# Branch hints, two final splits in other buffers, and all outputs from SyncE: an edge-convolution GNN on one core

## The chip, the cores and the metric

The kernel runs on one core of a Trainium2 chip. The metric is the device time of one execution in microseconds (us). The execution that was profiled is one of the runs; its span, from the first to the last instruction of the core, is a little shorter than its device time.

## The reference

A graph network with pre-normalisation over N = 2500 nodes with D = 256 features and E = 80,000 edges sorted by target node. There are three layers, then one product of all four feature sets with `Wf`, and the input is added at the end.

```python
def edge_conv(x, src, dst, W, b):
    m = concat([x[dst], x[src] - x[dst]]) @ W + b
    return segment_sum(m, dst) / maximum(segment_count(dst), 1)

h = maximum(layernorm(x), 0); xs = [h]
for W, b in ((W0, b0), (W1, b1), (W2, b2)):
    h = relu(edge_conv(h, src, dst, W, b)); xs.append(h)
out = x + concat(xs) @ Wf + bf          # Wf is 1024 x 256
```

## The kernel before

The program has two parts. `by_windows` does the whole computation under the assumption that the edges of a window of nodes fit into a fixed number of slots; it also writes a flag, `missing`, that says whether an edge was left out. Afterwards `gnn_kernel` loads the flag on every engine (`nc.values_load`, line 1425) and a branch on it (`tc.If`, line 1426) leads into `general`, a slower way of computing everything, or past it. With these inputs the flag is zero, so every engine jumps over the instructions of `general`, waits until what it issued is done, and meets the others at the barrier that ends the program (line 1450).

In `by_windows` the nodes are 20 tiles of 128. Edge counts are made as a dense matrix in five column groups, and a layer is a product of that matrix with the features. Most engine calls go through the helper `InOrder`, which keeps each engine's instructions in the order of the source; that is why nearly all of them carry line 282. A float32 operand that needs full precision is held as three reduced-precision parts (`high`, `low`, `across`). `Split` makes these parts for the two node tiles 2q and 2q+1 of `hT`: ScalarE (ACT) writes `high`, VectorE (DVE) makes `low` with a subtraction and `across` with a scalar_tensor_tensor. `Forms` does the like for a weight; `times` multiplies a split with the forms, 6 matmuls for a node tile. The parts lie in a pool `stage` with four buffers (tiles named "staged"), or, for the first layer, in the pool `ready` with seven buffers of half that size, from which `block()` also hands out the blocks of the count matrix that the layers multiply with (tiles named "block").

The part around the change is the end of the last layer and the final product:

- Each layer after the first runs a stream of 70 steps; after step n the function `tick(n)` slips other work in. In the last layer it makes four splits (steps 49, 56, 63 and 65) and the forms of the last part of `Wf` (64 to 67).
- The final loop runs over `order = [8, 9, 0, 1, 2, 3, 7, 6, 5, 4]`, whose entries q are pairs of node tiles; `i` counts them. For each pair TensorE (PE) writes both tiles' products into PSUM: 12 matmuls from a split, or 8 plain float32 matmuls for q = 2 and 7 (`PLAIN`). DVE then adds each tile to `acc` (`add_to_acc`), and SyncE (SP) issues the transfer of the tile to the output in HBM. In the last two pairs (`i >= Q - 2`) ACT issues the second tile's.
- At the end of round i the loop makes the splits of the next three entries that are not there yet. In effect the split of q = 3 comes after round 2, of 6 after round 4, of 5 after round 5 and of 4 after round 6. Each takes a `stage` buffer, which an earlier split must have freed.

The transfers go through eight semaphores in turn (100, 102, 103, 104, 106, 107, 109, 110). After the branch SP waits for each of these, then for a list of other semaphores, then goes to the barrier. DVE, PE and ACT wait after the branch for their own last instruction only. The barrier is led by GpSimd (POOL).

Of the kernel before, what the change touches and what calls it, by code (L numbers as in the profile page):

```python
# [8 lines left out]
F32 = mybir.dt.float32  # L9
I32 = mybir.dt.int32  # L10
AF = mybir.ActivationFunctionType
# [260 lines left out]
class InOrder:  # L272


    def __init__(self, tc, engine):
        self.tc, self.engine = tc, engine
# [37 lines left out]
def by_windows(ctx: ExitStack, tc: tile.TileContext, x, src, dst, Ws, bs, Wf, bf, out, missing):  # L314
    nc = tc.nc
    PE, DVE, ACT, POOL, SP = nc.tensor, nc.vector, nc.scalar, nc.gpsimd, nc.sync
    PEo, DVEo, POOLo, ACTo, SPo = (InOrder(tc, e) for e in (PE, DVE, POOL, ACT, SP))
    P = 128
    N, D = x.shape
# [4 lines left out]
    L = len(Ws)  # L324
    DC = D // P
# [22 lines left out]
    Q = NT // 2  # L348
# [23 lines left out]
    def bank():  # L372
        return ps[-1].tile([P, 512], F32, name="bank")


    acc = const.tile([P, NT, D], F32, name="acc")
    hT = const.tile([P, DC, NP], F32, name="hT")
# [66 lines left out]
    def load_wb(l, queue=SP):  # L444
        new_raw(l)
        ws[l] = (wts[l] if l == 1 else wpool.tile([P, DC, D], F32, name="wt")), raws[l][:, :, 0, :]
        queue.dma_start(ws[l][1], Ws[l][D:2 * D, :].rearrange("(c p) d -> p c d", p=P))
# [3 lines left out]
    def load_wt(l, queue=SP):  # L451
        queue.dma_start(wts[l] if l == 1 else ws[l][0], Ws[l][0:D, :].rearrange("(c p) d -> p c d", p=P))

    def load_wf(l, queue=SP):
        if l == L:
            new_raw(l)
        wfs[l] = raws[l][:, :, 1, :]
        queue.dma_start(wfs[l], Wf[l * D:(l + 1) * D, :].rearrange("(c p) d -> p c d", p=P))
# [22 lines left out]
    def load_b(l, queue=SP):  # L481
        queue.dma_start(brow[PAD:PAD + 1, l % 2, :], bs[l].rearrange("(o d) -> o d", o=1))
# [110 lines left out]
    parts = {}  # L593
# [320 lines left out]
    order = """  # L914
# [39 lines left out]
    DOWN = 1.0 - 0.5 / E12  # L954

    splits, coming = {}, []

    def block():
        return ready.tile([P, 2, 512], F32R, name="block")

    def flat(l):
        return raws[l].rearrange("p c t d -> p c (t d)") if l < L else wfs[l]

    class Split:

        def __init__(self, q, parts):
            h = hT[:, :, 2 * q * P:(2 * q + 2) * P]
            high, low, across = self.parts = [p.rearrange("p (c n) -> p c n", c=DC) for p in parts]
            ACTo.activation(high, h, AF.Copy, scale=DOWN)
            DVEo.tensor_sub(low, h, high.bitcast(F32))  # L970
            DVEo.scalar_tensor_tensor(across, low.bitcast(F32), -E12, high.bitcast(F32), op0=OP.mult, op1=OP.add)
            splits[q] = self

    class Forms:

# [35 lines left out]
    def split_own(g, c):  # L1011
# [4 lines left out]
        DVEo.tensor_sub(low, h, high.bitcast(F32))  # L1016
        DVEo.scalar_tensor_tensor(across, low.bitcast(F32), -E12, high.bitcast(F32), op0=OP.mult, op1=OP.add)

    def first_forms():
        DVEo.tensor_sub(ws[1][0], ws[1][0], ws[1][1])  # L1020
        yield
        coming.append(Forms(flat(1), [flat(1)[:, c, :] for c in range(DC)]))
        coming[0].high()
        coming[0].low()
        yield
        coming[0].across()
        coming[0].last()
        yield
        for q in range(2):
            two = [block().rearrange("p c n -> p (c n)") for _ in range(2)]  # L1030
            Split(q, [two[0][:, :2 * D], two[0][:, 2 * D:], two[1][:, :2 * D]])
            yield
        for t in range(0, NT, 5):
            DVEo.tensor_add(acc[:, t:t + 5, :], acc[:, t:t + 5, :], bf_sb.unsqueeze(1).to_broadcast([P, 5, D]))
            yield
# [68 lines left out]
    def combine(to, x):  # L1104
        DVEo.tensor_sub(to[:, M3:S5 + 1, :], x[:, 1::2, :], x[:, 0:2, :])
        DVEo.tensor_sub(to[:, S2, :], to[:, M3, :], x[:, 3, :])
        DVEo.tensor_add(to[:, M4, :], to[:, S2, :], x[:, 2, :])
# [10 lines left out]
    def add_to_acc(t, po):  # L1118
        DVEo.scalar_tensor_tensor(acc[:, t, :], po, share[:, t:t + 1], acc[:, t, :], op0=OP.mult, op1=OP.add)
# [161 lines left out]
    def load_alone(k, order):  # L1281
        c = order[2 * k] // 2
        st = stage.tile([P, 8 * GS], BF16, name="staged").rearrange("p (t n) -> p t n", n=GS)[:, :4, :]
        SPo.dma_start(st, a_dram[alone][:, 4 * c:4 * c + 4, :])
        loaded[k] = st
# [42 lines left out]
    PLAIN = (2, 7)  # L1328
    LAG = 2
    orders = [None, list(range(Q)), [8, 9, 0, 1, 2, 3, 7, 6, 5, 4], [8, 9, 0, 1, 2, 3, 7, 6, 5, 4]]  # L1330
    def split(q):
        tile_ = stage.tile([P, 4 * GS], F32R, name="staged")
        Split(q, [tile_[:, k * 2 * D:(k + 1) * 2 * D] for k in range(3)])

    for l in range(1, L):
        order = orders[l]
        lone = Alone(l, order)
        if l == 1:
            load_alone(0, order)
            split(order[2])  # L1340
        pending = []
        stream = Stream(l)
        for i in range(Q + LAG):
            if 0 < i <= Q:
                lone.make(i - 1)
            if i < Q:
                q = order[i]
                n = Nodes(l, q)
                n.multiply(splits.pop(q), coming[0])
                if i + AHEAD_H < Q and i % 2 == 1:  # L1350
                    load_alone((i + 1) // 2, order)
                n.parts()
                n.combine()
                if i + AHEAD_H < Q and order[i + AHEAD_H] not in splits:
                    split(order[i + AHEAD_H])
                pending.append(n)
            if i and pending:
                pending.pop(0).sums()
            if 0 < i <= DC:
                lone.own(i - 1, 0)  # L1360
            if i >= LAG:
                lone.multiply(i - LAG)
            if i == Q - 1:
                load_alone(Q // 2 - 1, order)
                stream.load(3)
        stream.make(2)
        lone.end()
        turn_of[1] = 0
        if l + 1 < L:
            load_b(l + 1, SPo)  # L1370
            load_wb(l + 1, SPo)
            load_wt(l + 1, SPo)
        load_wf(l + 1, SPo)
        after = orders[l + 1]

        def tick(n):
            if n == 3:
                combine(wsum, ws[l][0].rearrange("p c (o n) -> p (c o) n", o=2))
            if n == 40 and l + 1 < L:
                DVEo.tensor_sub(ws[l + 1][0], ws[l + 1][0], ws[l + 1][1])  # L1380
            if n in (49, 56):
                split(after[(n - 49) // 7])
            if n == 63 and l + 1 < L:
                load_alone(0, after)
            if n in ((65,) if l + 1 < L else (63, 65)):
                split(after[2 + (65 - n) // 2])
            if n == 64:
                raw = flat(l + 1)
                coming[:] = [Forms(raw, [raw[:, c, :] if l + 1 < L else raws[L][:, c, 0, :] for c in range(DC)])]
                coming[0].high()  # L1390
                coming[0].low()
            if n == 66:
                coming[0].across()
            if n == 67:
                coming[0].last()

        stream.run(tick)

    order = orders[L]
    for i, q in enumerate(order):  # L1400
        po = bank()
        po = [po[:, :D], bank()[:, :D] if i == Q - 1 else po[:, D:]]
        for k in range(2):
            if q in PLAIN:
                for c in range(DC):
                    PEo.matmul(po[k], hT[:, c, (2 * q + k) * P:(2 * q + k + 1) * P], wfs[L][:, c, :],
                               start=(c == 0), stop=(c == DC - 1))
            else:
                times(po[k], splits[q], k, coming[0])
        for k in range(2):  # L1410
            t = 2 * q + k
            add_to_acc(t, po[k])
            n = P if t < NT - 1 else LAST
            (ACTo if i >= Q - 2 and k else SPo).dma_start(out[t * P:t * P + n, :], acc[:n, t, :])
        for k in order[i + 1:i + 4]:
            if k not in splits and k not in PLAIN:
                split(k)


def gnn_kernel(tc: tile.TileContext, x, src, dst, Ws, bs, Wf, bf, out):  # L1420
    nc = tc.nc
    with tc.tile_pool(name="flag", bufs=1) as flag:
        missing = flag.tile([1, 1], I32, name="missing")
        by_windows(tc, x, src, dst, Ws, bs, Wf, bf, out, missing)
        again = nc.values_load(missing, min_val=0, max_val=1)
        with tc.If(again > 0):
            general(tc, x, src, dst, Ws, bs, Wf, bf, out)


# [26 lines left out]
```

## Time and profile before

| what | value |
|---|---|
| median device time, 3 runs | 478.93 us (478.14 to 479.45) |
| profiled execution, device time | 478.33 us |
| its span | 476.4 us |
| mean granted TensorE clock | 0.995 |
| PE busy | 463.5 us, 97% of the span |
| DVE busy | 380.9 us, 80% |
| ACT busy | 310.8 us, 65% |
| transfers `out_dram<-acc` issued by SP, by ACT | 18, 2 |
| last DVE addition ends | 468.3 us |
| from there to the end of the span | 8.1 us |

The profile tells engine time by groups of instructions. An engine name with a q (ACTq, SPq, PEldq) is that engine's sequencer: branches, semaphore waits, register loads and the issue of transfers, which are not counted as busy. Times within the span are counted from its first instruction.

### The profile page before, as it was taken

To read this page: it belongs to the slowest core of one execution; us is meant where nothing else is said; L and a number is where in the kernel's file an instruction comes from. 1 tells how busy PE (TensorE), PEld (TensorE's weight loads), DVE (VectorE), ACT (ScalarE), POOL (GpSimd) and SP (SyncE) were. 2 spreads that over 40 slices of the span, in tenths; PEclk is the share of its full clock that TensorE was granted. 3 is DMA by queue.
4 is the path that set the end of the run, shared out by engine and by line. 5 is a ranking of instruction groups with operands and counts; after the bars stand their busy time and mean duration, and the time that the engine had idled before them with its cause. 6 is when DMAs were issued, how large, how long until landed. Compare 5 with 4: busy or idle time off the path is not lost.

```text
span 476.4 us, 7357 instructions
## 1 busy us (share of the span) xinstructions
PE 463.5 (97%) x2739; PEld 365.9 (77%) x2739; DVE 380.9 (80%) x699; ACT 310.8 (65%) x543; POOL 42.7 (9%) x66
## 2 busy tenths in 40 slices
PE   8999999999999999999999999999999999999992
PEld 4787888787877888868887867877788787687691
DVE  8988988799898872599986848876999685669883
ACT  5776687685754441577869858766877886587330
POOL 2664014300101001000000000000000000000000
PEclk9999999999999999999999999999999999999997
DMA  8310084990824608441187542011124764120032
GB/s 279 96 46 1 1 163 70 193 216 14 178 42 89 131 1 179 95 131 43 45 291 258 182 160 89 1 44 45 43 54 158 289 207 151 77 88 0 1 128 95
DMA packets 21779, 52.11 MB, mean 109 GB/s; under 512 B 1943, under 2 KB 12134, under 8 KB 21734
## 3 DMA queue, kind: packets, MB, share of 16 engines
q1 hardware_dynamic: 14662, 33.67, 21.5%
q0 software_dynamic: 5856, 16.51, 18.1%
q10 hardware_dynamic: 1216, 1.37, 0.9%
q8 instruction: 23, 0.38, 0.3%
q14 instruction: 22, 0.18, 0.1%
HBM read 36.08 MB, written 15.46 MB: 108 GB/s over the span
## 4 chain that ended last, share of the span: by engine, by line
PE 86%; DVE 7%; POOL 2%; DMA 2%; issue 1%; SPq 0%; DVEq 0%; POOLq 0%
PE bank L282 82%; PE pz L282 3%; DVE acc L282 2%; DMA acc<-in_x_dram 2%; POOL acc L282 1%; DVE staged L282 1%; DVE st L282 1%; POOL es L282 1%; DVE zl L282 0%; POOL ed L282 0%; DVE mv L282 0%; DVE tmp L282 0%; PE turned L282 0%; DVE rs L282 0%; DVE kn L282 0%
## 5 line engine op out<-in xcount | busy, mean ns | idle before, releaser
L282 ACT CAST block<-staged 128x1008 fp32r<-128x1008 bf16 x120 | 117.8, 1032 | 17.1 <-DVE staged L282 6.3
L282 PE MATMUL bank<-block,zh 128*128 128x504 f32 (+1 forms) x200 | 83.7, 419 | 0.0
L282 PE MATMUL bank<-a,zh 128*128 128x504 f32 (+1 forms) x200 | 81.7, 409 | 0.0
L282 ACT CAST a<-bank 128x480 fp32r<-128x480 f32 (+1 forms) x105 | 54.5, 561 | 39.0 <-PE bank L282 37.1
L282 PE MATMUL bank<-a,zl 128*128 128x504 f32 (+1 forms) x200 | 77.8, 389 | 0.0
L282 PE MATMUL bank<-block,zl 128*128 128x504 f32 (+1 forms) x200 | 77.3, 387 | 0.0
L282 DVE TENSOR_TENSOR one_m<-iota_m,key_m 128x2048 bf16<-128x2048 bf16 (+2 forms) x55 | 64.3, 1169 | 9.9 <-PE bank L282 9.7
L282 PE MATMUL bank<-block,sh 128*128 128x504 f32 x160 | 69.0, 431 | 0.0
L282 PE MATMUL bank<-block,staged 128*128 128x512 f32 (+1 forms) x312 | 67.2, 365 | 0.6 <-DVE staged L282 0.5
L282 PE MATMUL bank<-block,sl 128*128 128x504 f32 x160 | 62.6, 391 | 0.0
L282 PEld LDWEIGHTS bank<-block,staged 128*128 128x128 f32 x312 | 52.3, 188 | 11.9 <-DVE staged L282 2.1
L282 DVE TENSOR_TENSOR one_n<-iota_n,key_n 128x960 bf16<-128x960 bf16 (+2 forms) x110 | 51.4, 508 | 0.0
L282 DVE TENSOR_TENSOR block<-staged 128x1008 fp32r<-128x1008 bf16 x40 | 46.9, 1204 | 5.5 <-PE bank L282 4.2
L282 PEld LDWEIGHTS <-one_m 128*128 128x128 bf16 x834 | 37.4, 97 | 13.6 <-issue 7.6
L282 PEld LDWEIGHTS bank<-block,zh 128*128 128x128 f32 x200 | 37.6, 188 | 10.8 <-issue 2.5
L282 PEld LDWEIGHTS bank<-block,zl 128*128 128x128 f32 x200 | 37.6, 188 | 10.6 <-issue 3.5
L282 PE MATMUL bank<-one_n,one_m 128*128 128x120 bf16 x834 | 44.7, 204 | 0.1
L282 PEld LDWEIGHTS bank<-a,zh 128*128 128x128 f32 x200 | 37.8, 189 | 6.4 <-issue 0.2
L282 PEld LDWEIGHTS bank<-a,zl 128*128 128x128 f32 x200 | 37.8, 189 | 6.3 <-issue 0.2
L282 DVE TENSOR_TENSOR staged<-staged 128x1008 bf16<-128x1008 bf16 x40 | 27.1, 678 | 17.3 <-ACT block L282 16.9
L282 PE MATMUL pz<-wbf,hT 128*128 128x256 f32 x160 | 38.7, 387 | 0.9 <-DMA wbf<-in_L_gnn_Wf_dram 0.7
L282 PEld LDWEIGHTS bank<-block,sh 128*128 128x128 f32 x160 | 30.1, 188 | 10.4 <-issue 3.5
(163 smaller groups left out, 611.8 us busy)
## 6 DMA issues: line engine op xcount, KB each, us to landing
staged<-a_dram SPq DMA_DIRECT2D x52, 504.0 KB, 4.2
a_dram<-a POOLq DMA_DIRECT2D x20, 630.0 KB, 10.8
out_dram<-acc SPq DMA_DIRECT2D x17, 128.0 KB, 1.7
acc<-in_x_dram POOLq DMA_DIRECT2D x3, 640.0 KB
wbf<-in_L_gnn_Wf_dram SPq DMA_DIRECT2D x4, 256.0 KB
acc<-in_x_dram SPq DMA_DIRECT2D x1, 896.0 KB
acc<-in_x_dram ACTq DMA_DIRECT2D x1, 768.0 KB
wbf<-in_L_gnn_W_dram SPq DMA_DIRECT2D x3, 256.0 KB, 6.6
```

The source lines that it names most:

```text
L282: return self.tc.keep_in_program_order(call(*args, **kwargs))
```

## The change

Three things change, and nothing in what is computed.

1. At the head of the program a branch hint for the branch on `missing` is put on PE, DVE and ACT. It is one instruction on each, ahead of all their other work, and says that the jump past `general` is likely. SP and POOL get none.
2. The final splits come sooner. The one for q = 6 is begun in step 68 of the last layer's stream (only ACT's `high`); its DVE part follows after round 0. The split of 3 is made after round 1, of 5 after round 2 and of 4 after round 3. Those of 6 and 3 no longer lie in `stage` but take two `ready` blocks each, as the first layer's two splits do.
3. SP issues all 20 output transfers; ACT issues none.

```diff
-        def __init__(self, q, parts):
-            h = hT[:, :, 2 * q * P:(2 * q + 2) * P]
-            high, low, across = self.parts = [p.rearrange("p (c n) -> p c n", c=DC) for p in parts]
-            ACTo.activation(high, h, AF.Copy, scale=DOWN)
-            DVEo.tensor_sub(low, h, high.bitcast(F32))
+        def __init__(self, q, parts, whole=True):
+            self.h = hT[:, :, 2 * q * P:(2 * q + 2) * P]
+            self.parts = [p.rearrange("p (c n) -> p c n", c=DC) for p in parts]
+            ACTo.activation(self.parts[0], self.h, AF.Copy, scale=DOWN)
+            if whole:
+                self.rest()
+            splits[q] = self
+
+        def rest(self):
+            high, low, across = self.parts
+            DVEo.tensor_sub(low, self.h, high.bitcast(F32))
             DVEo.scalar_tensor_tensor(across, low.bitcast(F32), -E12, high.bitcast(F32), op0=OP.mult, op1=OP.add)
-            splits[q] = self
...
+    def split_in_blocks(q, whole=True):
+        two = [block().rearrange("p c n -> p (c n)") for _ in range(2)]
+        return Split(q, [two[0][:, :2 * D], two[0][:, 2 * D:], two[1][:, :2 * D]], whole)
...
         def tick(n):
+            if n == 68 and l + 1 == L:
+                begun.append(split_in_blocks(6, False))
...
-            (ACTo if i >= Q - 2 and k else SPo).dma_start(out[t * P:t * P + n, :], acc[:n, t, :])
-        for k in order[i + 1:i + 4]:
-            if k not in splits and k not in PLAIN:
-                split(k)
+            SPo.dma_start(out[t * P:t * P + n, :], acc[:n, t, :])
+        if i == 0:
+            begun[0].rest()
+        elif i == 1:
+            split_in_blocks(3)
+        elif i < 4:
+            split((5, 4)[i - 2])
...
+        tc.mark_branch_hint_location("again", "LikelyTaken",
+                                     engines=[getattr(mybir.EngineType, e) for e in ("PE", "DVE", "Activation")])
         by_windows(tc, x, src, dst, Ws, bs, Wf, bf, out, missing)
         again = nc.values_load(missing, min_val=0, max_val=1)
-        with tc.If(again > 0):
+        with tc.If(again > 0, label="again"):
             general(tc, x, src, dst, Ws, bs, Wf, bf, out)
```

More of the change, by code (lines that the diff above doesn't have):

```diff
@@ L1029, in first_forms @@
         for q in range(2):
-            two = [block().rearrange("p c n -> p (c n)") for _ in range(2)]
-            Split(q, [two[0][:, :2 * D], two[0][:, 2 * D:], two[1][:, :2 * D]])
+            split_in_blocks(q)
             yield
@@ L1333, in split @@
         Split(q, [tile_[:, k * 2 * D:(k + 1) * 2 * D] for k in range(3)])
+    begun = []
     for l in range(1, L):
```

## The prediction

> **What bounds the kernel now.** I read the page's totals first, then the windows over the end, then the timeline of the last 25 us, then the source rows of the branch (lines 1425, 1426) and of the closing barrier (line 1450), then the output transfers.
>
> ```profile
> span 476.4 us, 7357 instructions
> PE 463.5 (97%) x2739; PEld 365.9 (77%) x2739; DVE 380.9 (80%) x699; ACT 310.8 (65%) x543; POOL 42.7 (9%) x66
> ...
> PE 86%; DVE 7%; POOL 2%; DMA 2%; issue 1%; SPq 0%; DVEq 0%; POOLq 0%
> ```
>
> PE is full, so only work on PE's path or idle time at the ends can matter. The change touches no matmul, so I look at the end, in windows (the column after the length is PE's busy time, DVE's is the third):
>
> ```profile
> 462.30:467.50 5.20, 4.91 (x38) 4.48 (x36) 5.13 (x12) 0.00 (x0) 0.00 (x0) 1.00 0.35 117
> 467.50:468.40 0.90, 0.00 (x0) 0.00 (x0) 0.83 (x3) 0.00 (x0) 0.00 (x0) 1.00 0.85 264
> 468.40:476.40 8.00, 0.00 (x0) 0.00 (x0) 0.00 (x0) 0.00 (x0) 0.00 (x0) 0.69 0.21 69
> ```
>
> For the last 8 us no engine computes. Just before, DVE has no idle time and PE a little. The timeline shows the cause: PE's last pair waits for the split of q = 4, which stands behind additions on DVE, and then DVE ends with six additions.
>
> ```profile
> 465.29 0.69 DVE L282 SCALAR_TENSOR_TENSOR staged<-staged 128x512 fp32r<-128x512 f32 x1
> 465.90 2.43 DVE L282 SCALAR_TENSOR_TENSOR acc<-bank,share,acc 128x256 f32<-128x256 f32 x6
> 466.03 1.46 PE L282 MATMUL bank<-block,staged 128*128 128x256 f32 x10 [0.28 <-DVE staged L282]
> ```
>
> The empty 8 us are in the source rows of the branch and the barrier (ns min/median/max, first and last start):
>
> ```profile
> L1426 PEldq COMPARE_BRANCH  x1: 3942/3942/3942, 466.7 to 466.7; - x1
> L1426 DVEq COMPARE_BRANCH  x1: 72/72/72, 468.2 to 468.2; - x1
> L1426 ACTq COMPARE_BRANCH  x1: 54/54/54, 470.1 to 470.1; - x1
> ...
> L1426 DVEq EVENT_SEMAPHORE  x1: 21/21/21, 471.3 to 471.3; - x1
> L1426 ACTq EVENT_SEMAPHORE  x1: 17/17/17, 473.2 to 473.2; - x1
> ```
>
> ```profile
> L1450 SPq DRAIN  x3: 7/7/7, 473.3 to 475.8; - x3
> ...
> L1450 ACTq DRAIN  x2: 8/72/135, 475.4 to 475.8; - x2
> ```
>
> The next instruction after a taken branch comes 3.9 us later on PE, 3.0 on DVE, 3.1 on ACT. ACT needs another 2.2 us to its drain (473.24 to 475.45); of the transfers on the instruction queues one begins in that gap, at 473.84. So ACT reaches the barrier last, at 475.58; the span ends 0.83 us later. ACT is late because it branches last: it issues two outputs until 469.48 and only then loads the flag. SP waits for the landings and is held by ACT's semaphore for 0.4 us; without ACT it would drain at 472.98.
>
> The outputs are late too:
>
> ```profile
> L282 SPq DMA_DIRECT2D out_dram<-acc x18: 286/356/1506, 454.1 to 468.0; - x18
> L282 ACTq DMA_DIRECT2D out_dram<-acc x2: 372/742/1111, 467.6 to 468.4; - x2
> ...
> DMA to landing us min/median/max: 1.7/1.7/1.8
> ```
>
> ```profile
> q8 instruction: 1, 0.02, 4.5%
> ```
>
> An issue takes about 0.36 us, the last on each queue 1.51 and 1.11; both return at 469.48. The second fence is the DMA view of 467.5 to 469.5: PE's jump fetches 16 KB of code, from 467.63 to 469.08 in the single transfer records. For the outputs on semaphores 110 and 100 fifteen of sixteen parts land at 468.6 and 469.1, the sixteenth only at 470.35 and 470.63. One DMA engine is held up by the code. The last output lands at 471.81. The same shows twice in midstream: SP's load at 385.97 (code transfer at 385.51) took 1.29 us and that at 417.63 (417.14) 1.02, where its like take 0.43.
>
> **The change part by part.** The sum stands against the profiled execution: span 476.41, device time 478.33, which is 0.60 below the median of 478.93.
>
> *ACT's two issues move to SP.* ACT loses two issues and two waits. Its last work is then `high` of q = 4, which waits for PE's second round (454.9). So it branches near 456 to 460 and, with 5.3 us for branch and second fetch as now, is at the barrier before 466. What is late next is SP. Its part, 475.58 - 472.98 = 2.60 us, goes. For SP two issues are added: back to back they cost 0.43 to 0.48 (466.40, 466.83, 467.31); I take 0.46. Behind them on SP stands only its own branch, and the barrier waits for that.
>
> *Splits sooner.* A split costs DVE 1.32 us (457.19 to 458.51), a pair of additions 0.79 (459.56 to 460.35); neither count nor kind changes. From the first addition at 453.54 DVE now runs: pair 0, rest of 6, pair 1, split 3, pair 2, split 5, pair 3, split 4, done at 453.54 + 4 x 0.79 + 4 x 1.32 = 461.98; then pairs 4 to 7 to 465.14. PE needs split 3 at 459.2 (done 457.8), 6 at 462.3 (455.7), 5 at 463.9 (459.9) and 4 at 465.4 (462.0): no wait is left. PE loses its stall, 0.44 us between two matmuls that otherwise start 0.12 apart and 0.1 at the next: PE's end 467.49 becomes 466.95. The last addition then starts at 466.98 rather than 467.86 and ends at 467.46, 0.87 us sooner. ACT's `high` of 6 (0.63) now stands between the two Relus of 1.05; behind it the second ends at 454.8 and `high` of 3 at 455.4, while DVE takes that at 456.4: hidden by 1 us; without that cover 0.63 at most. The PSUM bank of the very last tile must be freed by pair 4 (462.8, needed at 466.0). In the buffers of 6 and 3 lay blocks of steps 66 to 69, read by 451.9; `high` of 6 starts at 453.2: no wait there.
>
> *All outputs on SP.* Twelve follow one another from 462.5: 462.5 + 11 x 0.46 = 467.56; the last addition ends at 467.46, so both fit. Undisturbed it lands 1.72 later, 469.28. But PE still branches: earlier by its stall, at 466.2, and its code transfer starts 0.96 us later, 467.2. Now 467.63 to the last landing at 471.81 is 4.18 us with five outputs behind the code; after, four outputs (issued from 466.18) stand behind it, and one is 8 packets of 46 ns = 0.37 on the held engine: 467.2 + 3.81 = 471.0. Bounds 469.3 (no hold) and 471.5 (twelve issues in a row push further); I take 471.0, since three rows show the hold. Gain 0.8 us.
>
> *The hints.* No row shows one. Their own cost lies between 0 and a sequencer instruction of 17 to 51 ns (the semaphore rows); ACT's stands before the load of `dst`, with which the first chain begins: I take 0.05 us. Their gain could be up to 3.9, 3.0 and 3.1 us for the three engines, but with ACT early the barrier waits for SP: DVE, branching at 467.4, would reach it at 470.5 without a hint and SP at about 472. And for the landings little is won: before, each engine began another code transfer 0.6 to 0.7 us after it resumed (PE 470.62, transfer 471.32). If PE's jump is instant, that one starts at 466.2 + 0.3 + 0.65 = 467.15, when the other would have. So 0 at the end from hints, bounds -6.9 and +1.6.
>
> [...]
>
> **Sum:** 2.60 + 0.8 - 0.05 = 3.4 us (3.35). Span 473.0, device time 474.9, on the median's footing 478.93 - 3.4 = 475.5.
>
> **Rivals.**
> *A, the outputs are free.* With the hints PE's code comes early and the next fetch does not start, or sits on another engine. Then the last landing is 469.3, SP's list and drain take 1.2 us and the barrier 0.83, and the span ends at about 471.4: 5.0 us, 473.9. For it: the hints are on just the engines that fetched at the end. Against: the second transfers after each resumption.
> *B, slower.* The hinted code takes the place of the next sequential block early on. PE then waits a whole jump, 3.9 us, at its first crossing (about 20 us in), and DVE or ACT 3.0 in the same opening phase, which PE waits for. 6.9 lost against 3.4 won: 482.4. It decides from 4.8 us lost; one stall alone gives 479.4. For it: the hint stands very far ahead. Against: PE crosses 21 blocks without any idle time that the page counts.
> *C, SP's branch.* SP has four more instructions. Now its branch costs at most 1.07 us (469.58 to 470.65, a landing). If its target were outside what is loaded, 469.6 + 3.0 for the jump, 1.3 for its list and 0.9 to the end of the barrier give a span of 474.8: 477.3, at the edge of no change.
> *D, the hints do nothing.* That is the same 475.5.
>
> **How the numbers follow.** My case, D included: 0.62 (474.7 to 476.4). A: 0.22. C and like losses: 0.08. B: 0.08. The range 473.4 to 477.7 takes in A, the first case and most of C's neighbourhood. 0.3% is 1.4 us, about what a measurement of this kernel can tell from no change, so faster means below 477.5: first case and A, some of C: 0.86; same 0.06; slower 0.08.
>
> **What would show it.** ACT's branch before 461 and its drain before 467; DVE's last addition ending near 467.5; no PE idle from staged after 460; SP issuing 20 outputs, with one or two near the end still over 1 us, and the last landing near 471; SP drains last. DVE's first instruction after its branch within 0.5 us means that hints work. A longest issue below 0.5 us and a landing near 469.3 mean A. A PE gap of 3 us in the first 40 us means B; SP's first wait 3 us behind its branch, C.

## The result and the profile after

The changed kernel takes 475.55 us (median of 8 runs, 474.83 to 476.04); the kernel before, run beside it, 477.77 us (8 runs, 477.14 to 479.45). The ratio is 0.9945, with a 95% interval of 0.9933 to 0.9958: faster by 0.55%, some 2.6 us. The profiled execution took 475.97 us, with a span of 474.0 us against 476.4 before.

The totals, two rows of the queues and the shares of the chain, from the page of the changed kernel:

```profile
span 474.0 us, 7362 instructions
...
PE 462.7 (98%) x2739; PEld 365.3 (77%) x2739; DVE 380.5 (80%) x699; ACT 310.6 (66%) x543; POOL 42.6 (9%) x66
...
q8 instruction: 22, 0.36, 0.3%
q14 instruction: 19, 0.16, 0.1%
...
PE 88%; DVE 5%; POOL 3%; DMA 2%; issue 1%; ACTq 0%; DVEq 0%; POOLq 0%
```

PE's work is unchanged (2739 matmuls). The chain ends with DVE's last addition, so it says nothing of the last 6 us. The queue q8 is taken as PE's code queue: in the profile before, its last two transfers start 0.96 us into PE's branch (467.63) and 0.70 us after the branch ended (471.32). It carried 23 transfers of 16 KB before, the first at 21.57 us, and carries 22 now.

The source rows of the branch (line 1442 now), with the duration in ns, then the start:

```profile
L1442 ACTq COMPARE_BRANCH  x1: 68/68/68, 456.1 to 456.1; - x1
L1442 ACTq EVENT_SEMAPHORE  x1: 17/17/17, 457.0 to 457.0; - x1
L1442 PEldq COMPARE_BRANCH  x1: 398/398/398, 465.8 to 465.8; - x1
L1442 PEldq EVENT_SEMAPHORE  x1: 51/51/51, 467.5 to 467.5; - x1
L1442 DVEq COMPARE_BRANCH  x1: 84/84/84, 468.1 to 468.1; - x1
L1442 DVEq EVENT_SEMAPHORE  x1: 21/21/21, 468.7 to 468.7; - x1
```

From the end of the branch to the next instruction it is now 0.9 us on ACT (3.1 before) and 0.5 on DVE (3.0); PE's branch takes 398 ns where it took 3942, and what PE then waits for until 467.5 is its own last matmul. The hints work, although they stand at the very head of the program (0.7 to 0.8 us). These are the rows of the closing barrier, the three hints among them, since they carry its line:

```profile
L1466 SPq DRAIN  x3: 7/7/7, 473.1 to 473.4; - x3
L1466 ACTq DRAIN  x2: 8/8/8, 457.1 to 473.4; - x2
...
L1466 ACTq BRANCH_PREFETCH_HINT  x1: 45/45/45, 0.7 to 0.7; - x1
L1466 DVEq BRANCH_PREFETCH_HINT  x1: 51/51/51, 0.8 to 0.8; - x1
L1466 PEldq BRANCH_PREFETCH_HINT  x1: 50/50/50, 0.8 to 0.8; - x1
```

ACT drains at 457.1, 18 us earlier than before. SP is the last to drain (its second, at 473.17). The windows over the end (PE's busy time follows the length, DVE's is the third) and the timeline's row of the last matmuls from a split show that PE is full until its end, and that DVE, which had no idle time there before (5.13 of 5.20 us), now has 0.5 us of it:

```profile
462.30:467.50 5.20, 5.13 (x41) 4.83 (x39) 4.69 (x13) 0.00 (x0) 0.00 (x0) 1.00 0.65 212
467.50:468.00 0.50, 0.00 (x0) 0.00 (x0) 0.46 (x1) 0.00 (x0) 0.00 (x0) 1.00 0.34 111
468.00:474.00 6.00, 0.00 (x0) 0.00 (x0) 0.00 (x0) 0.00 (x0) 0.00 (x0) 0.84 0.28 93
```

```profile
464.44 2.99 PE L282 MATMUL bank<-block,staged 128*128 128x256 f32 x24
```

PE's wait for `staged` is gone: the row has no bracket. What is left is 6 us in which no engine computes. Two views tell why it is not less, the output transfers and the DMA view of 466.9 to 468.7:

```profile
L282 SPq DMA_DIRECT2D out_dram<-acc x20: 287/386/2093, 454.5 to 470.2; - x20
...
DMA to landing us min/median/max: 1.8/1.9/2.0
```

```profile
q8 instruction: 1, 0.02, 5.6%
```

SP's issues take 0.3 to 0.7 us, all but one: that of 466.85 returns only at 468.94. PE's jump is over at 466.20, and 0.76 us later, from 466.96 to 468.57, its queue fetches one more block of code. Of the outputs on semaphores 109 and 110, fifteen of sixteen parts land by 467.65 and 468.15, the sixteenth at 469.75 and 470.07. So one part of each comes 2.1 and 1.9 us after the rest, 1.2 and 1.5 us after the code is through; before, on 110 and 100, it was 1.7 and 1.5 us after the rest. This is the hold; that one DMA engine, busy with the code, causes it is the author's reading of the one part in sixteen. Three more issues follow the blocked one on SP, the last output lands at 472.00, and SP's list, drain and barrier take the rest.

### The profile page after: what moved, and what is told of

The parts are those of the page before. It is cut to its first block, busy times and chain, and to the rows that moved or that the text cites. A ratio compares the mean times of both kernels' runs of the same rounds, so it can differ in the third digit from the quotient of the medians.

```text
span 474.0 us, 7362 instructions
## 1 busy us (share of the span) xinstructions
PE 462.7 (98%) x2739; PEld 365.3 (77%) x2739; DVE 380.5 (80%) x699; ACT 310.6 (66%) x543; POOL 42.6 (9%) x66
## 4 chain that ended last, share of the span: by engine, by line
PE 88%; DVE 5%; POOL 3%; DMA 2%; issue 1%; ACTq 0%; DVEq 0%; POOLq 0%
PE bank L282 84%; PE pz L282 3%; DMA acc<-in_x_dram 2%; DVE acc L282 2%; POOL acc L282 1%; DVE st L282 1%; POOL es L282 1%; POOL ed L282 1%; DVE staged L282 1%; DVE tmp L282 0%; DVE zl L282 0%; DVE mv L282 0%; PE turned L282 0%; DVE kn L282 0%; DVE rs L282 0%
## 5 line engine op out<-in xcount | busy, mean ns | idle before, releaser
L282 PE MATMUL bank<-block,staged 128*128 128x512 f32 (+1 forms) x288 | 63.5, 371 | 0.3 <-DVE staged L282 0.2
L282 PEld LDWEIGHTS bank<-block,staged 128*128 128x128 f32 x288 | 49.2, 188 | 11.4 <-DVE staged L282 1.6
```

Of the source, the lines that this page charges most:

```text
L282: return self.tc.keep_in_program_order(call(*args, **kwargs))
```

## The experiments

The theory was the one that these views suggest: the end is set by SP's outputs, these are held by the code that PE fetches behind its jump, and the hints spare the jump but not that fetch. It has two rivals: that the hints bring nothing, because ACT left the barrier's end by issuing no outputs; and that the held sixteenth part is the outputs' own doing, twelve close transfers in a row. All runs were timed in five rounds beside the kernel before on the same chip; the table is in the order of the text.

| kernel | median us (runs) | kernel before | ratio, 95% interval |
|---|---|---|---|
| e1_no_hints | 475.96 (9) | 477.42 | 0.9973, 0.9961 to 0.9985 |
| e2_hints_only | 475.49 (5) | 477.42 | 0.9959, 0.9945 to 0.9972 |
| e3_sp_only | 476.71 (11) | 477.42 | 0.9983, 0.9969 to 0.9996 |
| e4_splits_only | 476.85 (11) | 477.42 | 0.9987, 0.9978 to 0.9996 |
| r_after (changed kernel) | 474.94 (6) | 477.30 | 0.9943, 0.9929 to 0.9957 |
| r_no_hints (e1 again) | 476.17 (12) | 477.30 | 0.9973, 0.9962 to 0.9985 |
| e7_act_issues | 474.97 (6) | 477.72 | 0.9934, 0.9922 to 0.9946 |
| e9_pe_dve_hints | 474.95 (6) | 477.30 | 0.9946, 0.9933 to 0.9960 |
| e5_late_pe | 476.50 (7) | 477.72 | 0.9972, 0.9961 to 0.9983 |
| e8_after_landing | 473.22 (5) | 477.30 | 0.9909, 0.9895 to 0.9924 |
| e12_landing_no_hints | 475.52 (5) | 477.25 | 0.9962, 0.9948 to 0.9976 |
| e10_pairs | 472.58 (4) | 477.25 | 0.9900, 0.9884 to 0.9916 |

**One part at a time.** The first kernel is the changed one without its hints.

```diff
-        tc.mark_branch_hint_location("again", "LikelyTaken", engines=[...])
...
-        with tc.If(again > 0, label="again"):
+        with tc.If(again > 0):
```

> The changed kernel without its three hints. Theory (hints are worth nothing at the end, SP's landings set it): within 0.5 us of the changed kernel, 2.2 to 3.2 us below the kernel before; PE's branch takes 3.9 us again, its code transfer starts about 467.2 and holds the last outputs just as now, DVE resumes 3.0 us after its branch. Rival (the hints carry the gain): less than 1 us below the kernel before.

It keeps half of the gain, 1.3 us of 2.6, between the two figures of the expectation. So the hints are worth something beside the other two parts.

The second is the kernel before with nothing but the hints.

> The kernel before with nothing but the three hints; ACT still issues two outputs. Theory: the 2.6 us were ACT's late jump and its second fetch, so a short jump of ACT wins them as well: ACT drains near 471, SP ends last near 473, 2.3 to 2.7 us below the kernel before. Rival (the hints are too far from the branch, or ACT waits for something other than code): no change, within 0.5 us.

It gains 2.0 us, a little less than the 2.3 expected at the least. The rows of its branch (line 1428) show ACT still branching last, at 470.1, behind its two outputs, but not late any more:

```profile
L1428 ACTq COMPARE_BRANCH  x1: 68/68/68, 470.1 to 470.1; - x1
L1428 ACTq EVENT_SEMAPHORE  x1: 17/17/17, 470.6 to 470.6; - x1
```

ACT drains at 470.63 (475.45 before), and SP is last at 472.76. In the profile a hint thus removes the 2.60 us that ACT cost at the barrier, without moving an issue. That the medians show only 2.0 may lie in the profile of the kernel before: at 478.33 us it stands 0.9 above the median of the 25 runs beside this kernel.

The third is the kernel before with all outputs on SP.

```diff
-            (ACTo if i >= Q - 2 and k else SPo).dma_start(out[t * P:t * P + n, :], acc[:n, t, :])
+            SPo.dma_start(out[t * P:t * P + n, :], acc[:n, t, :])
```

> The kernel before with nothing but all 20 outputs on SP; no hints, splits as before. Theory: ACT jumps early and hides its fetches, 2.6 us go, but SP now issues its last outputs one after another behind the held engine and gives 0.3 to 1 us back: 1.6 to 2.4 us below the kernel before. Rival (the gain needs the hints): within 0.5 us of the kernel before.

A miss: 0.8 us by the ratio, well below what was expected. Its times fall into two groups, four from 474.81 to 475.45 and seven from 476.64 to 477.70. The profiled one (475.45) belongs to the lower group, and there the expected thing happened: 2.0 us below the median of the kernel before. Its outputs show the hold:

```profile
L282 SPq DMA_DIRECT2D out_dram<-acc x20: 286/382/1800, 453.7 to 469.8; - x20
...
DMA to landing us min/median/max: 1.7/1.8/3.6
```

What the other seven paid 1.2 to 2.2 us more for was not profiled. In the profiled one, PE's second code transfer starts only at 471.15, when the last output is nearly through (it lands at 471.58).

The fourth is the kernel before with the sooner splits alone (`rest`, `split_in_blocks` and the schedule as in the change; no hints, ACT keeps two issues).

> The kernel before with nothing but the sooner splits; ACT still issues two outputs, no hints. Theory: DVE's last addition ends 0.87 us sooner, but the held engine and ACT's jump set the end as before; ACT's last issue returns 0.3 to 0.6 us sooner: 0.2 to 0.8 us below the kernel before. Rival (the additions set the end): 0.9 us or more below.

It gains 0.6 us. The last addition ends at 467.10 instead of 468.33. PE ran 0.36 us ahead of before's times from the first 40 us on, so the splits' part of that is 0.87 us, as expected. ACT's drain, at 474.0, is still the last (line 1464), and the jumps (line 1440) are longer than before:

```profile
L1440 DVEq COMPARE_BRANCH  x1: 72/72/72, 467.6 to 467.6; - x1
L1440 ACTq COMPARE_BRANCH  x1: 54/54/54, 468.3 to 468.3; - x1
...
L1440 ACTq EVENT_SEMAPHORE  x1: 17/17/17, 471.9 to 471.9; - x1
L1440 DVEq EVENT_SEMAPHORE  x1: 21/21/21, 472.0 to 472.0; - x1
```

```profile
L1464 ACTq DRAIN  x2: 8/72/136, 474.0 to 474.4; - x2
```

DVE's jump takes 4.4 us here, 3.0 before, and ACT's 3.6, 3.1 before. The DMA view of 468.9 to 469.7 has three code transfers on q14 and one on q8 within 0.8 us. That these four fall together may be why; no run tests it:

```profile
q14 instruction: 3, 0.02, 8.5%
q8 instruction: 1, 0.02, 7.8%
```

Splits alone 0.6 and SP alone 0.8 make 1.4, against 1.3 for both; the hints bring 2.0 alone and 1.3 on top of both. Within the intervals the first two add, and the hints share part of their gain with them.

**How sure the hints' share is.** The changed kernel and e1 were run again on one chip.

> The changed kernel once more, beside the next three on one chip: 2.2 to 3 us below the kernel before. PE's first matmuls should again run 0.2 to 0.4 us later by the 40th than without hints, as in all four hinted profiles so far, if the hints at the head cost that.

> The changed kernel without hints once more. The prediction's theory (hints are worth nothing at the end): within 0.5 us of the changed kernel. Rival that the first run suggests (without a hint PE fetches code twice in the last 8 us, once for the jump and once behind it, and each holds outputs): 0.8 to 1.6 us above the changed kernel, with two transfers on PE's code queue after 465 and a wider spread of times.

The ratios repeat (0.9943 and 0.9973): the hints are worth 1.2 us by the medians, 1.4 by the ratios. The DMA view of r_no_hints for 464 to 471 shows what the unhinted kernel has and the hinted one has not, a second block of PE's code. The rows of the outputs follow, first without hints, then r_after with them:

```profile
q8 instruction: 2, 0.03, 2.2%
```

```profile
L282 SPq DMA_DIRECT2D out_dram<-acc x20: 332/398/1391, 453.7 to 468.5; - x20
```

```profile
L282 SPq DMA_DIRECT2D out_dram<-acc x20: 287/390/2355, 453.7 to 469.6; - x20
```

The first block comes during PE's jump (465.92, 1.32 us; the branch takes 3562 ns from 465.0), the second 0.8 us after PE resumed (469.44, 1.10 us). Without hints one issue of SP is blocked for 1.39 us, and then the output on semaphore 104 has fifteen parts by 470.61 and its last at 471.76, 1.2 us after the second block is through. With hints one issue is blocked for 2.36 us, and no part of the last output is late (in the first profile of this kernel its sixteen land from 471.80 to 472.00). This profile's last output lands 0.4 us behind that of r_after (471.40), not 1.3, and the profiles of e1 and of the changed kernel's first runs are like it: with the difference at the start taken off, e1's span is 0.4 us the longer. So the second fetch is shown, and with it 0.4 us of the price. The profiled run of r_no_hints (475.71) lies below its median and that of r_after (475.32) above. What the slower executions without hints pay beyond that was not profiled and stays open.

The expectation of r_after for the start failed: its 40th matmul is 0.06 us later than before's, not 0.2 to 0.4, though in the first profile of the changed kernel it was 0.35 later. Late in the kernel the start's difference to before was +0.49 and -0.39 in the two profiles of the same code, and from -0.60 to +0.34 in the others, hinted or not. Only 0.09 us at the first matmul belongs to the hints in every profile; the rest is not settled.

**Does ACT matter beside the hints?** In the next kernel ACT issues the second output of the last two pairs again, as before the change; in the one after it only ACT's hint is missing.

```diff
-            SPo.dma_start(out[t * P:t * P + n, :], acc[:n, t, :])
+            (ACTo if i >= Q - 2 and k else SPo).dma_start(out[t * P:t * P + n, :], acc[:n, t, :])
```

> The changed kernel, hints and sooner splits kept, but with ACT issuing the second output of each of the last two pairs as before. Theory: with a hint ACT's jump is short, so this costs no 2.6 us; the two queues wait for the held engine side by side and not one after the other: 0 to 0.8 us below the changed kernel. Rival (ACT's issues cost their late jump even with the hint): 1 to 2.6 us above the changed kernel.

```diff
-                                     engines=[getattr(mybir.EngineType, e) for e in ("PE", "DVE", "Activation")])
+                                     engines=[getattr(mybir.EngineType, e) for e in ("PE", "DVE")])
```

> The changed kernel without ACT's hint; PE's and DVE's stay. ACT issues no output and jumps before 460, so its long jump should cost nothing at the end. Theory A (ACT's hint, ahead of its load of dst, costs the 0.3 us at the start): 0.1 to 0.4 us below the changed kernel, PE's 40th matmul as early as without hints. Theory B (the start only varies, or PE's and DVE's hints cost it): the same time within 0.2 us, the start still late.

The rows of the first one's branch:

```profile
L1442 ACTq COMPARE_BRANCH  x1: 68/68/68, 468.9 to 468.9; - x1
L1442 ACTq EVENT_SEMAPHORE  x1: 17/17/17, 469.4 to 469.4; - x1
```

Neither clearly differs from the changed kernel (0.9934 and 0.9946 against 0.9943 to 0.9945). In the first, ACT branches at 468.89, resumes at 469.37 and drains at 469.46, 2.6 us before SP. So these runs show no gain of all outputs on SP once ACT has a hint, and none of ACT's hint once ACT issues no outputs. Either will do. On the start, the kernel without ACT's hint gives a mixed answer: its 40th matmul is early (0.04 us before that of the kernel before), as theory A had it, but its time is the same, and of two later kernels with all hints e8 has that matmul at +0.14 and e10 at -0.14.

**Does the fetch hold the outputs?** If so, PE must jump later. The first attempt put 16 matmuls behind PE's last ones.

```diff
+    pad = bank()
+    for _ in range(16):
+        PEo.matmul(pad[:, :D], hT[:, 0, :P], wfs[L][:, 0, :], start=True, stop=True)
```

> The changed kernel with 16 extra plain matmuls of PE behind its last product, whose results nobody reads: 3.4 us more work on PE, so that its jump and the next code transfer come after the last outputs are on their way. Theory (the code transfer holds one DMA engine and with it the last landings): SP's longest issue falls from 2.1 to below 0.8 us, the last output lands near 470.0 rather than 471.9, and the span is 1.3 to 2.0 us shorter although PE works longer. Rival (the outputs are slow for their own sake, or PE's end matters): the same time or up to 3 us longer.

A miss: PE itself ended last, so the run cannot price the hold. The timeline has 32 records for the 16 plain float32 matmuls; they took 7.1 us, and PE ended at 474.2:

```profile
467.12 7.07 PE L282 MATMUL bank<-wbf,hT 128*128 128x256 f32 x32
```

Besides, a transfer on PE's code queue started at 467.66, with PE's weight loads running until 473.8 and its branch still to come, and it fell on the outputs in place of the other (one SP issue took 1.24 us).

The second attempt lets DVE and PE wait, not work. A memset writes one element of a tile of `acc` that an output reads, so it must wait for that output to land; a 1x1 matmul reads the element. The tile chosen, 11, is the third from the end to go out (the expectation says the fourth). Both engines then load the flag and jump when the outputs are nearly through.

```diff
+    DVEo.memset(acc[:1, 11, 0:1], 0.0)
+    pad = bank()
+    PEo.matmul(pad[:1, :1], acc[:1, 11, 0:1], acc[:1, 11, 0:1], start=True, stop=True)
```

> The changed kernel with two tiny instructions at its end: DVE clears one element of acc tile 11 once that tile's output has landed (the fourth output from the end), and PE multiplies it, so that DVE and PE load the flag and jump only after most outputs have left. Theory (the code transfer behind PE's jump holds the last outputs): SP's longest issue falls from 2.1 to below 0.6 us, the last output lands 1.5 to 2.3 us sooner against PE's last product, and the time is 1.2 to 2.2 us below the changed kernel. Rival (the outputs queue for their own sake): the same time, or up to 1 us longer for the added wait.

```profile
468.36 0.06 DVE L282 MEMSET acc<- 1x1 f32 x1 [1.30 <-DMA out_dram<-acc]
...
468.48 0.18 PE L282 MATMUL bank<-acc 1*1 1x1 f32 x2 [1.94 <-DVE acc L282]
```

```profile
L282 SPq DMA_DIRECT2D out_dram<-acc x20: 332/398/732, 453.7 to 467.4; - x20
```

```profile
q1 hardware_dynamic: 1421, 1.29, 64.8%
q14 instruction: 1, 0.01, 0.6%
```

It is 1.7 us faster than the changed kernel on the same chip (473.22 against 474.94), though two engines wait on purpose. Of PE's code nothing is fetched between 464 and 470 (the last view); the next block comes at 470.22. No issue is blocked near the end: the eight from 464.0 on take 3.86 us in all. No sixteenth part is late, and the last output lands at 469.25. There are as many outputs as close together, so the hold was the code's doing, not theirs. DVE's jump was put off together with PE's and was not tested by itself; in the changed kernel the blocked issue (466.85 to 468.94) coincides with PE's code transfer (466.96 to 468.57) and with none of another engine. The five times lie within 0.21 us.

The counter-test is the same kernel without the hints.

> The kernel that jumps after the landing of tile 11, but without any hint. Theory (a jump without a hint takes 3 to 4 us, which only an early jump hides): PE, jumping near 469, reaches the barrier near 473 and now ends last: 2 to 3.2 us above the kernel with hints, 0.7 to 2.2 us below the kernel before. Rival (hints only matter through the code transfer that holds the outputs): within 0.5 us of the kernel with hints.

```profile
L1444 PEldq COMPARE_BRANCH  x1: 3978/3978/3978, 468.9 to 468.9; - x1
L1444 DVEq EVENT_SEMAPHORE  x1: 21/21/21, 471.7 to 471.7; - x1
L1444 PEldq EVENT_SEMAPHORE  x1: 51/51/51, 472.9 to 472.9; - x1
```

These rows of its branch show PE on its way from 468.9 to 472.9. The outputs are free (last issue 467.2, last landing 469.0), but SP's list contains DVE's and PE's last semaphores, and SP stands at these two for 1.80 and 1.20 us, until 473.0. It gives back 2.3 us by the medians, 2.5 by the ratios. So it is the hints that make a late jump cheap: PE's branch takes 3978 ns here, 393 in e8.

**The best version.** To e8 one thing is added: in rounds 4 to 7 both tiles of a pair go out in one transfer of 256 KB.

```diff
-            SPo.dma_start(out[t * P:t * P + n, :], acc[:n, t, :])
+            if 3 < i < 8:
+                if k:
+                    SPo.dma_start(out[(t - 1) * P:(t + 1) * P, :].rearrange("(k p) d -> p k d", p=P), acc[:, t - 1:t + 1, :])
+            else:
+                SPo.dma_start(out[t * P:t * P + n, :], acc[:n, t, :])
```

> The kernel that jumps after the landing of tile 11 (hints kept), with the outputs of rounds 4 to 7 issued as one transfer of 256 KB for each pair of tiles. Theory (with the hold gone SP's own pitch is late: its last issue came 0.35 us after the last addition): the last issue follows the addition at once and 0.2 to 0.4 us go, 4.2 to 4.6 below the kernel before. Rival (the larger transfers fill the DMA engines just before the end): the same time or up to 0.4 us more than without pairs.

```profile
L282 SPq DMA_DIRECT2D out_dram<-acc x16: 283/372/405, 453.5 to 466.9; - x16
```

16 issues instead of 20, and the last begins at 466.91 instead of 467.44. SP drains at 469.58 instead of 470.42, and the span is 470.4. Of these 0.84 us, 0.2 are an earlier start and 0.36 the sooner last landing. The remaining 0.28 are an accident of the count: the last output now lies on semaphore 110, the last of the eight that SP waits for, where in e8 it lay on 104 with four more waits behind it. The kernel takes 472.58 us, 4.7 below the kernel before, slightly more than expected; that it beats e8 (0.9900 against 0.9909, with intervals that overlap) is likely, not shown.

## Why the prediction was right, and where it was not

The time, 475.5, the direction and the range held. The closeness is in good part luck, twice over. Without hints the two parts that were to bring 3.4 us bring 1.3, and the hints, put at 0, bring about as much again: the sum was 0.8 us too large by the ratio (a gain of 2.6), 1.2 by the medians (2.2). It was taken off a median of 478.93; over eight runs the kernel before has 477.77, so the starting point was 1.2 too high as well.

- **ACT's issues, 2.60 us: there in the profiles, mis-sized for the median run, and too narrow in the cause.** ACT drains at 457.13 and SP is last. On before's clock (the profile of after lies 0.49 us later from about 30 us on) the last engine reaches the barrier 2.9 us sooner: these 2.60, and the 0.3 of the last landing below. But e2 has the same without moving an issue. Timed alone, the move brings 0.8 us (e3; 2.0 in the faster group), and beside the hints these runs show no gain from it (e7). The term came from one profile of the kernel before, an execution of 478.33 us, 0.6 to 1.1 above the median of each later set of its runs.
- **Splits sooner: right.** On before's clock the last addition ends at 467.47; 467.46 was predicted. PE's stall is gone, and the cover for ACT's `high` and for the PSUM bank held.
- **The last landing, predicted 0.8 us sooner: mis-sized, 0.3.** The working had the fetch at 467.2 and four outputs behind it. PE branched sooner than forecast, so its fetch came at 466.47 on before's clock and had six outputs behind it (the two on 109 and 110 and the four after them). The working also left out that the hold blocks SP itself: one issue of 2.09 us, with three more behind it on the same queue. On before's clock the last output lands at 471.51 instead of 471.81, and SP drains at 472.68 instead of the 472.98 it would have without ACT.
- **The hints, predicted 0: mis-sized, 1.2 to 1.4 us, inside the bound of +1.6.** The step said that the fetch behind the jump takes the place of the jump's own at about the same time, so that nothing is won. For one transfer that is what happened, 0.76 us after the jump. But without hints PE fetches twice within the last 8 us, and in the profiles of e1 and r_no_hints the second holds the last output. That accounts for 0.4 us; the rest is measured by the medians alone, and its cause is open. The times of the unhinted kernels that issue all outputs from SP range over 2.7 to 3.1 us (e1, e3, r_no_hints), those of the hinted changed kernel over 1.2 and 0.9.
- **The hints' own cost, 0.05: 0.09 us at the first matmul.**
- **What a hint does to the jump.** The branch's own record tells little on ACT and DVE: 50 to 72 ns without a hint, 68 to 90 with one. The next instruction follows 2.4 us (ACT in e12 and r_no_hints) to 4.4 us (DVE in e4) later without a hint, and 0.4 us (ACT in e7) to 0.9 us (ACT in the changed kernel) with one. On PE the record itself went from 3942 to 398 ns, with the hint 21 code transfers ahead.
- **The rivals.** A, free outputs, did not come, since the fetch behind the jump did start; e8, with that fetch put off, has its last landing at 469.25 (469.65 on before's clock), near A's figure of 469.3. B, a stall early: behind the first matmul no hinted profile has a gap above 1.1 us in PE's opening, where B had 3. C, SP's branch: its first wait follows within 0.5 us of the branch. D, hints that do nothing: refuted.

## What to carry to other kernels

Here an unhinted branch past unused code took 2.4 to 4.4 us on PE, DVE and ACT, and beside PE's last code transfers one part in sixteen of some of the last outputs was 1.5 to 2.1 us late (before and changed kernel). Where a program ends like this one, give the engines that branch late a hint, even at the head of the program, and let them jump only when the outputs are nearly through: here that is worth 1.7 us beyond the change itself, and it needs the hints. Judge such an edit by its whole set of runs: the times of one kernel spread by up to 3 us here, and one profile shows only one of these cases.

## What the runs showed of the hardware

- A branch hint at the head still works 21 code blocks later on PE: its branch took 0.39 to 0.40 us (398 ns in the changed kernel, 393 in e2 and e8) where it took 3.56 to 3.98 without one (3562 in e1 and r_no_hints, 3822 in e4, 3942 before, 3978 in e12). PE's code queue carries one transfer fewer than in the kernel before (22 against 23) and none near the hint (its first starts at 21.90 us), so these traces do not show when the target was loaded. A hint nearer to its branch was not tried.
- Behind the hinted jump PE fetched one more block 0.76 us after the jump, in the changed kernel (466.96) and in e8 (470.22).
- A PE code transfer among the last outputs (1.44 us before, 1.62 in the changed kernel) came with one late sixteenth of outputs then on their way: on 110 and 100 before, on 109 and 110 in the changed kernel. It also came with a blocked issue of SP: 1.51 us before, 2.09 in the changed kernel, 1.39 in r_no_hints, 2.36 in r_after.
